# A third dA buffer, a different access pattern for two silu passes, and new due times in the scan stage of a four-layer image kernel

## The chip, the cores and the metric

The kernel runs as one program on one core of a Trainium2 chip. The metric is the device time of one execution in microseconds. Three runs of the kernel before took 7575.3, 7574.78 and 7561.64 us; the median is 7574.78 us.

The engines are named as in the profile: PE (TensorE, matrix products into PSUM), DVE (VectorE), ACT (ScalarE), POOL (GpSimd) and SP (SyncE, which here only issues DMAs). Each engine works through its own instructions in order.

## The reference

Four layers act on an image batch of 4 x 64 x 128 x 128 in float32. Layers 0 to 2 (a spectral gate with attention, a Fourier mixing block with experts, a Hartley convolution with blur) are not touched. Layer 2 ends with a mask that leaves 65 of the 128 columns nonzero. Layer 3 runs two selective scans over the result, one along the whole image ("spa", 65536 steps), one over the channels of each pixel ("spe", 8 steps for each of 65536 pixels), normalises each by groups, and adds them to the input:

```python
xi, z = split(x @ in_w.T)
xc = silu(conv(xi) + conv_b)
dt, B, C = split(xc @ xproj_w.T);  dt = softplus(dt @ dt_w.T + dt_b)
dA = exp(dt[..., None] * A);  dBx = dt[..., None] * B * xc[..., None]
h = dA_t * h + dBx_t          # scan over t, 16 states for each of 128 channels
y = sum_s(h * C_t) + xc * D
out = (y * silu(z)) @ out_w.T
...
spa = silu(group_norm(ys)) + x;  spe = x + silu(group_norm(ye))
return spa * w[0] + spe * w[1] + x
```

## The kernel before

Layer 3 is cut into chunks: 65 "spe" chunks of 512 tokens (64 pixels by 8 steps), one short chunk ("run") that follows the scan through 60 zero inputs, and 4 x 19 "spa" chunks of up to 483 tokens (7 image rows of 69 columns: 65 kept ones, and four in which the run of masked columns is held as constants). Every chunk has eight steps, one for each row group q, in the order `ORDER = (0, 2, 4, 6, 1, 3, 5, 7)`; the place of a group in it is called k below. A row group puts 16 channels x 8 states on the 128 partitions; the other 8 states lie behind them in the free dimension (`sg` 0 and 1).

One step is: two exponentials on ACT write dA (`do_exp`, L1490); the product of dt, x and B is written into the tile `hd` (`do_dB`, L1518), by DVE for k = 0, 2, 3, 5, 7 and by POOL for k = 1, 4, 6; DVE scans `hd` in place with dA (`do_scan`, L1525 for spe, L1529 and L1535 for spa); POOL multiplies the result with C (`do_hc`, L1564; in spe one instruction for two steps). PE sums the products over the states into the PSUM tile `ps_y` (`do_sums`), and once for each chunk DVE multiplies this with silu(z) (`do_y`, L1605).

dA has two buffers, both in PSUM and each of two banks; they alternate from step to step (`self.turn`). With two banks for the tile `m`, one for `y` and one for `dx`, PSUM is full.

Work of a chunk that comes ahead of its steps: `do_x` (L1415 to L1417) makes xc and zs by two silu passes, which need another table of ACT's functions than the exponentials, so a table load stands in front of them and another behind them. In spe chunks PE writes the result by steps, and the silu passes read PSUM in order and write SBUF with a step of 8 elements. `do_dt` computes softplus on ACT and PE, `do_bc` and `do_keep` make B and C, `do_put` and `do_copy` send dt and dt*x through DRAM to spread the rows over the partitions. The tiles xc and zs have three buffers each.

In spa chunks, the scan overwrites the columns of `hd` that stand for the masked run, and `keep_run` (L1680 to L1682, on ACT) writes them back from the saved tile `e_run`, in two pieces: k = 0 to 3 and k = 4 to 7.

From the second image on, eight spa chunks of each image also carry a part of the previous image's `combine`: DMAs in, two silu passes in place (part 1, L1819 and L1820), matmuls that add the three terms, copies out of PSUM and DMAs out; the last image's combine follows the scans. `affine` prepares its factors once for each image.

The order on PE, DVE, ACT and POOL is written out by hand: `scans` gives every piece of work a due time in steps (8 to a chunk, relative to the chunk's first step), sorts by it and emits in this order. A piece due at 2.3 stands on each engine behind all pieces due earlier. The DMA issues on SP are placed by the compiler's scheduler. Waits follow from the data: who reads a tile waits for its writer, and who writes a buffer waits for its last reader.

Of the kernel before, what the change touches and what calls it, by code (L numbers as in the profile page):

```python
# [9 lines left out]
F32 = mybir.dt.float32  # L10
# [27 lines left out]
ORDER = (0, 2, 4, 6, 1, 3, 5, 7)  # L38
BY_DVE = (0, 4, 6, 3, 7)


# [273 lines left out]
class Net:  # L315
# [944 lines left out]
    def layer3(self, x2s, x2k, y1, ye):  # L1260
        tc, nc = self.tc, self.nc
        self.x2s, self.x2k, self.y1, self.ye = x2s, x2k, y1, ye
        with ExitStack() as ctx:
# [7 lines left out]
            nc.vector.memset(self.eps, 1e-5)  # L1271
            self.dA = [self.psum.tile([128, 1024], F32, name=f"dA{i}") for i in range(2)]
            self.const, self.small = const, pool("st", 2)
            self.work = pool("w", 2)
# [128 lines left out]
    def do_x(self, u):  # L1403
        nc, c, n = self.nc, u["c"], u["n"]
        spa = u["spa"]

        v = lambda t: t if spa else t.rearrange("p (t x) -> p t x", t=8)
        w = lambda t: t if spa else t.rearrange("p (x t) -> p t x", t=8)
        a0, a2 = u["taps"]
        p, pz = self.ps("m")[:, u["lo"] : n], self.ps("m")[:, u["lo"] : n]  # L1410
        self.mm(v(p), c["w0"], a0, stop=False)
        self.mm(v(p), c["w1"], a2, start=False)
        self.mm(v(pz), c["z"][64:128], a2[64:128])
        u["xc"], u["zs"] = self.tile2("xc", u, 3), self.tile2("zs", u, 3)
        nc.scalar.activation(w(u["xc"]), v(p), AF.Silu, bias=c["cb"])  # L1415
        nc.scalar.activation(w(u["zs"]), v(pz), AF.Silu)
        nc.scalar.preload_act_table_set("natural_log_exp_and_others")  # L1417
# [62 lines left out]
    def do_exp(self, u, q, sg):  # L1480

        t = (lambda x: x) if u["spa"] else (lambda x: x.rearrange("p (x t) -> p x t", t=8)[:, :, 1:8])
        a = u["c"]["a"][:, 2 * q + sg : 2 * q + sg + 1]
        if sg == 0:
            self.turn = 1 - self.turn
            u["dA", q] = self.dA[self.turn]
        at = (TOK + 1) * sg + 1 if u["spa"] else 512 * sg
        if u["kind"] == "run" and sg == 0 and q in ORDER[:2]:
            self.nc.vector.memset(u["dA", q][:, TOK + 1 : TOK + 2], 0.0)
        self.nc.scalar.activation(t(u["dA", q][:, at + u["lo"] : at + u["n"]]), t(u["dt", q]), AF.Exp, scale=a)  # L1490
# [180 lines left out]

    def keep_run(self, u, part):

        at = slice(4 * part, 4 * part + 4)
        runs = lambda sg: self.all[:, at, (TOK + 1) * sg + TOK + CW :: CW][:, :, :CR]
        if u["kind"] == "run":
            for sg, to in ((0, self.e_run[:, at]), (1, runs(1))):
                of = (TOK + 1) * sg + RUN
                of = self.all[:, at, of : of + 1]
                self.nc.scalar.copy(to, of.to_broadcast([128, 4, CR]) if sg else of)  # L1680
        self.nc.scalar.copy(runs(0), self.e_run[:, at].to_broadcast([128, 4, CR]))  # L1681

    def scans(self, us):
# [7 lines left out]
        for ci, u in enumerate(us):  # L1691
            do = lambda when, f, *a: todo.append((8 * ci + when, len(todo), f, a))
            spa = u["spa"]
            if spa:
                do(-22.0, self.spa_load, u)
            else:
                for part, when in enumerate((-2.9, 4.7, 6.42)):
                    do(when, self.do_first, u, part)
                m, i = divmod(u["at"], 4)
                do(-13.0, self.spe_taps, u)  # L1700
                for g in range(8 if i == 0 else 0):

                    if m:
                        do(-48.0 + 3 * g if m > 1 else -48.0, self.spe_load, m, g)
                for g in range(8 if i == 3 or u["at"] == chunks - 1 else 0):
                    do(12.3 + 3 * g, self.spe_store, m, g)
            do(-12.9, self.do_x, u)
            for part, when in enumerate((-11.65, -11.25, -10.65, -10.05, -9.8, -9.55, -9.3, -9.0, -8.05)):
# [6 lines left out]
            for i, when in enumerate((4.7, 4.74, 5.9, 9.42, 9.74) if u["kind"] != "run" else ()):  # L1715
                do(when, self.do_sums, u, i)
            for part in range(2 if spa else 0):
                do(4.1 * part + 4.6, self.keep_run, u, part)
            if u["kind"] != "run":
                do(10.76, self.do_y, u)  # L1720
                do(12.2, self.spa_out if spa else self.spe_out, u)
                do(13.64, self.do_stats, u)
        mine = [j for j in range(len(steps)) if not by_pool(j)]
        for j, (u, q) in enumerate(steps):
            do = lambda when, f, *a: todo.append((j + when, len(todo), f, a))
            do(-6.0, self.do_copy, u, q, "dt")
            do(-1.3, self.do_exp, u, q, 0)
            do(-1.0, self.do_exp, u, q, 1)
            if by_pool(j):
                do(-6.5, self.do_copy, u, q, "dx")  # L1730
                do(-4.22, self.do_dB, u, q, nc.gpsimd)
            else:
                do(-1.61, self.do_dB, u, q, nc.vector)
            do(0.3, self.do_scan, u, q)
            if u["kind"] != "run":
                do(0.77, self.do_hc, u, q)
# [4 lines left out]
        for ci, u in enumerate(us):  # L1741
            if u["kind"] == "spa" and u["at"][1] == SPC - 1:
# [3 lines left out]
                for i in range(8):  # L1746

                    for part, when in enumerate((4.0, 10.37, 16.3, 16.75, 16.8, 17.51)):
                        do(when + 8 * (i + 1), self.combine, b, i, part)
# [118 lines left out]
```

## Time and profile before

| what | value |
|---|---|
| median of three runs | 7574.78 us |
| the profiled execution's own time | 7564.79 us |
| its span, first to last instruction | 7562.9 us |
| busy share of the span: PE, DVE, ACT, POOL | 88%, 71%, 64%, 47% |
| granted TensorE clock, mean | 0.94 |
| first and last `do_y` (L1605) | 3640.58 and 7499.20 us |
| mean distance of two `do_y`, spe chunks | 27.33 us |
| the same, full spa chunks without combine | 26.37 us |
| the same, spa chunks with combine | 29.56 us |

The scan stage takes the second half of the span. `do_y` occurs once in each chunk, so the distance of two of its starts is the time of one chunk; the means are over 61 spe chunks (3640.58 to 5307.50 us), 36 spa chunks without and 24 with combine. The page's busy shares are averages over the whole span, most of POOL's work lies in this stage. Start-to-start distances are used for the cost of one instruction where they stand back to back, since neighbouring instructions overlap by a few hundredths of a microsecond.

### The profile page before, as it was taken

What the parts mean: (1) busy time and instruction counts of PE and PEld (TensorE: products, weight loads), DVE (VectorE), ACT (ScalarE), POOL (GpSimd) and SP (SyncE); (2) the same over time, 40 slices, a digit from 0 to 9 for tenths busy, and PEclk for the clock granted to TensorE, in tenths of its full rate; (3) what the DMA queues carried; (4) which work ended last, traced back from release to release, by engine and by line L of the source; (5) the groups of instructions that cost most, each with busy time, mean ns of one, the idle gap of its engine ahead of it and who ended that gap; (6) DMA issues with size and microseconds to landing.
All of it is one profiled execution on the core that took longest, in us unless ns stands there. A gap on an engine that the chain in (4) does not pass through costs nothing.

```text
span 7562.9 us, 105294 instructions
## 1 busy us (share of the span) xinstructions
PE 6622.1 (88%) x39058; PEld 2887.9 (38%) x39058; DVE 5344.1 (71%) x6633; ACT 4813.2 (64%) x7926; POOL 3524.4 (47%) x1648
## 2 busy tenths in 40 slices
PE   7998999989998999989888888888888788788786
PEld 6334553446334643446222222222222232232233
DVE  2665646563665556553898998889888888888886
ACT  2565536553655446443777777777777777787885
POOL 1000000000000000000899999999899789788795
PEclk9998999998998999988999999999999999999998
DMA  3000010001000200013455555554444454554554
GB/s 87 1 1 1 28 46 1 1 28 45 1 1 1 63 10 1 1 61 125 134 137 140 138 139 139 140 139 137 132 136 136 135 158 131 144 160 124 149 154 115
DMA packets 364098, 646.93 MB, mean 86 GB/s; under 512 B 46784, under 2 KB 219584, under 8 KB 362048
## 3 DMA queue, kind: packets, MB, share of 16 engines
q1 hardware_dynamic: 357680, 609.91, 29.1%
q10 hardware_dynamic: 5904, 30.28, 1.2%
q8 instruction: 308, 5.05, 0.3%
q14 instruction: 206, 1.69, 0.1%
HBM read 517.80 MB, written 122.22 MB: 85 GB/s over the span
## 4 chain that ended last, share of the span: by engine, by line
PE 56%; DVE 19%; ACT 11%; issue 7%; POOL 4%; DMA 3%; SPq 0%; DVEq 0%; POOLq 0%; ACTq 0%
PE ps_sp L333 13%; PE ps_m L333 12%; PE ps_s L333 7%; PE ps_o L333 6%; PE ps_dx L333 6%; DVE hd L1518 5%; DVE hd L1525 5%; PE ps_pt L333 4%; PE ps_y L333 4%; ACT dA L1490 3%; DVE hd L1529 3%; POOL hc L1564 2%; DMA big<-in_sr 2%; DVE big L1061 2%; ACT L1417 1%
## 5 line engine op out<-in xcount | busy, mean ns | idle before, releaser
L1564 POOL TENSOR_TENSOR hc<-hd,C 128x910 f32<-128x910 f32 (+3 forms) x868 | 2316.0, 2677 | 362.3 <-DVE hd L1529 147.5
L1529 DVE TENSOR_TENSOR_SCAN hd<-dA,hd 128x968 f32<-128x968 f32 (+1 forms) x576 | 1226.3, 2131 | 188.7 <-ACT dA L1490 185.9
L755 DVE TENSOR_REDUCE nmz<-ps_sp 128x1 f32<-128x320 f32 x2048 | 896.0, 485 | 621.6 <-PE ps_sp L333 612.4
L333 PE MATMUL ps_dx<-dtx,c_sel 128*128 128x483 f32 (+3 forms) x1420 | 796.1, 644 | 589.9 <-DVE hd L1518 589.5
L771 ACT ACTIVATE big<-ps_sp 128x512 f32<-128x512 f32 (+1 forms) x1536 | 830.6, 592 | 719.6 <-PE ps_sp L333 718.3
L1525 DVE TENSOR_TENSOR_SCAN hd<-dA,hd 128x1024 f32<-128x1024 f32 x520 | 1185.2, 2283 | 109.7 <-ACT dA L1490 100.5
L930 POOL TENSOR_TENSOR aw<-pack_a 128x128 f32<-128x128 f32 x8 | 3.5, 454 | 2192.4 <-PE ps_m L333 2192.4
L1518 POOL TENSOR_TENSOR hd<-s_dx,B 128x1024 f32<-128x1024 f32 (+5 forms) x450 | 956.4, 2126 | 95.1 <-ACT hd L1681 78.5
L333 PE MATMUL ps_sp<-uT,kT 32*128 32x512 f32 x3072 | 923.9, 648 | 1.4 <-ACT big L771 0.8
L1518 DVE TENSOR_TENSOR hd<-ps_dx,B 128x1024 f32<-128x1024 f32 (+5 forms) x750 | 810.9, 1081 | 33.2 <-PE ps_dx L333 31.7
L333 PE MATMUL ps_sp<-kT,qT 32*128 32x320 f32 x4096 | 817.4, 499 | 3.9 <-ACT qT L736 3.3
L1490 ACT ACTIVATE dA<-s_dt,c_spa_a 128x483 f32<-128x483 f32 (+3 forms) x1232 | 788.9, 645 | 44.9 <-DVE hd L1529 30.6
L1490 ACT ACTIVATE dA<-s_dt,c_spe_a 128x448 f32<-128x448 f32 x1040 | 652.0, 637 | 63.3 <-DVE hd L1525 51.5
L333 PEld LDWEIGHTS ps_dx<-dtx,c_sel 128*128 128x128 f32 x1420 | 230.8, 195 | 1079.5 <-DVE hd L1518 586.6
L333 PE MATMUL ps_y<-hc,c_sum 128*32 128x455 f32 (+3 forms) x4512 | 548.6, 556 | 3.2 <-POOL hc L1564 3.2
L333 PEld LDWEIGHTS ps_sp<-uT,kT 32*128 32x128 f32 x3072 | 278.8, 185 | 438.0 <-issue 242.7
L333 PE MATMUL ps_o<-big,va 128*32 128x512 f32 (+1 forms) x3072 | 414.3, 611 | 0.0
L333 PE MATMUL ps_s<-pack_a,big 128*64 128x128 f32 (+4 forms) x2832 | 371.6, 307 | 43.7 <-DMA big<-in_x 20.2
L333 PEld LDWEIGHTS ps_sp<-kT,qT 32*128 32x128 f32 x4096 | 358.2, 190 | 57.2 <-issue 36.6
L333 PEld LDWEIGHTS ps_s<-pack_a,big 128*128 128x128 f32 (+2 forms) x2832 | 330.0, 180 | 65.6 <-issue 26.2
L333 PE MATMUL ps_m<-xc,c_spa_bc 128*128 128x483 f32 (+3 forms) x616 | 313.1, 631 | 0.0
L1461 ACT COPY C<-ps_m 128x483 f32<-128x483 f32 (+4 forms) x284 | 159.5, 562 | 211.7 <-PE ps_m L333 210.9
(405 smaller groups left out, 10180.6 us busy)
## 6 DMA issues: line engine op xcount, KB each, us to landing
s_dt<-ddt SPq DMA_DIRECT2D x520, 256.0 KB
s_dt<-ddt SPq DMA_DIRECT2D x544, 241.5 KB
s_dx<-ddx SPq DMA_DIRECT2D x195, 256.0 KB
s_dx<-ddx SPq DMA_DIRECT2D x204, 241.5 KB
ddt<-dt SPq DMA_DIRECT2D x65, 256.0 KB
ddx<-dtx SPq DMA_DIRECT2D x65, 256.0 KB
A<-x2s SPq DMA_DIRECT2D x136, 121.2 KB
ddt<-dt SPq DMA_DIRECT2D x68, 241.5 KB
```

What stands on the lines that cost most here:

```text
L333: self.nc.tensor.matmul(out, lhsT, rhs, start=start, stop=stop)
L755: nc.vector.tensor_reduce(self.nmz[n % 2][:, j, at : at + 1], p[:, :KEYS], AX.X, ALU.max, negate=True)
L771: nc.scalar.activation(slot(m, 2 * wu + q)[rows], p[rows], AF.Exp)
L930: nc.gpsimd.tensor_tensor(aw[i], k(f"aw{i + 1}"), k("sg"), ALU.mult)
L1061: nc.vector.scalar_tensor_tensor(acc(i), y, gate[:, p : p + 1], acc(i), ALU.mult, ALU.add)
L1417: nc.scalar.preload_act_table_set("natural_log_exp_and_others")
L1461: self.nc.scalar.copy(u["BC"][k // 2][:, k % 2, u["lo"] : u["n"]], u["bc", k])
L1490: self.nc.scalar.activation(t(u["dA", q][:, at + u["lo"] : at + u["n"]]), t(u["dt", q]), AF.Exp, scale=a)
L1518: eng.tensor_tensor(v(dB[:, :, x:y]), v(d), v(u["BC"][0][:, :, x:y]), ALU.mult)
L1525: scan(hd[:, :1024], dA, hd[:, :1024], 0.0, ALU.mult, ALU.add)
L1529: scan(hd[:, :m], dA[:, :m], hd[:, TOK : TOK + m], 0.0, ALU.mult, ALU.add)
L1564: mul = lambda to, a, b: self.nc.gpsimd.tensor_tensor(to, a, b, ALU.mult)
```

## The change

A third dA buffer, in SBUF, is used at k = 4 (q = 1) alone; the other seven steps alternate between the two PSUM buffers, and the exponentials of k = 4 are emitted 0.95 steps earlier. In spe chunks the two silu passes write SBUF in order and read PSUM with a step of 64 elements. `do_x` is due 0.8 steps earlier, directly behind part 1 of `combine`, which is moved by 0.08 steps. `keep_run` has three pieces (k = 0-1, 2-4, 5-7) due at 2.6, 6.0 and 9.0 instead of two due at 4.6 and 8.7. `do_y` is due 0.57 steps later, the output matmul and copy 0.35 steps later, the output's DMAs of spe 0.35 later.

```diff
+AHEAD = 4
+KEEP = ((0, 2, 2.6), (2, 5, 6.0), (5, 8, 9.0))
...
             self.dA = [self.psum.tile([128, 1024], F32, name=f"dA{i}") for i in range(2)]
+            self.dA.append(const.tile([128, 1024], F32, name="dA2"))
...
-        w = lambda t: t if spa else t.rearrange("p (x t) -> p t x", t=8)
+        w = lambda t: t if spa else t.rearrange("p (t x) -> p x t", t=8)
+        o = lambda t: t if spa else t.rearrange("p (x t) -> p x t", t=8)
...
-        nc.scalar.activation(w(u["xc"]), v(p), AF.Silu, bias=c["cb"])
-        nc.scalar.activation(w(u["zs"]), v(pz), AF.Silu)
+        nc.scalar.activation(o(u["xc"]), w(p), AF.Silu, bias=c["cb"])
+        nc.scalar.activation(o(u["zs"]), w(pz), AF.Silu)
...
         if sg == 0:
-            self.turn = 1 - self.turn
-            u["dA", q] = self.dA[self.turn]
+            k = ORDER.index(q)
+            self.turn = self.turn if k == AHEAD else 1 - self.turn
+            u["dA", q] = self.dA[2 if k == AHEAD else self.turn]
...
-    def keep_run(self, u, part):
+    def keep_run(self, u, k0, k1):
...
-                do(-13.0, self.spe_taps, u)
+                do(-13.8, self.spe_taps, u)
...
-                    do(12.3 + 3 * g, self.spe_store, m, g)
-            do(-12.9, self.do_x, u)
+                    do(12.65 + 3 * g, self.spe_store, m, g)
+            do(-13.7, self.do_x, u)
...
-            for part in range(2 if spa else 0):
-                do(4.1 * part + 4.6, self.keep_run, u, part)
+            for k0, k1, when in KEEP if spa else ():
+                do(when, self.keep_run, u, k0, k1)
             if u["kind"] != "run":
-                do(10.76, self.do_y, u)
-                do(12.2, self.spa_out if spa else self.spe_out, u)
+                do(11.33, self.do_y, u)
+                do(12.55, self.spa_out if spa else self.spe_out, u)
...
-            do(-1.3, self.do_exp, u, q, 0)
-            do(-1.0, self.do_exp, u, q, 1)
+            early = 0.95 if j % 8 == AHEAD else 0.0
+            do(-1.3 - early, self.do_exp, u, q, 0)
+            do(-1.0 - early, self.do_exp, u, q, 1)
...
-                    for part, when in enumerate((4.0, 10.37, 16.3, 16.75, 16.8, 17.51)):
+                    for part, when in enumerate((4.0, 10.29, 16.3, 16.75, 16.8, 17.51)):
```

## The prediction

> **What bounds the kernel now.** I read the page's busy shares by slices first, since the change touches the scan stage alone, then busy times by window, then the chain of waits inside the stage, then single chunks on the timeline.
>
> ```profile
> DVE  2665646563665556553898998889888888888886
> ACT  2565536553655446443777777777777777787885
> POOL 1000000000000000000899999999899789788795
> ```
>
> From slice 20 on, DVE and POOL are both eight to nine tenths busy, ACT seven. The windows give busy microseconds (and instructions) of PE, PEld, DVE, ACT and POOL in 200 us of spe, of spa with combine and of plain spa:
>
> ```profile
> 3900.00:4100.00 200.00, 170.03 (x632) 57.28 (x632) 181.76 (x120) 153.20 (x235) 182.30 (x66) 0.97 0.52 141
> ...
> 6500.00:6700.00 200.00, 172.99 (x623) 65.90 (x625) 162.78 (x127) 168.17 (x264) 167.67 (x82) 0.94 0.62 170
> 6700.00:6900.00 200.00, 169.22 (x594) 56.99 (x590) 176.99 (x116) 157.31 (x269) 185.85 (x91) 0.96 0.50 141
> ```
>
> No engine is full: POOL and DVE lack a tenth each, in combine chunks a sixth. The waits of the stage say what for (total us, times, longest):
>
> ```profile
> DVE hd L1529 <- ACT dA L1490: 185.9, 200, 2.9
> DVE yz L1605 <- PE ps_y L333: 181.5, 139, 3.5
> ...
> POOL hc L1564 <- DVE hd L1529: 147.5, 162, 11.5
> ACT hd L1681 <- POOL hd L1518: 112.3, 65, 2.9
> POOL hc L1564 <- DVE hd L1525: 95.7, 54, 3.3
> DVE hd L1525 <- ACT dA L1490: 95.0, 133, 2.3
> ...
> POOL hd L1518 <- ACT hd L1681: 78.5, 60, 2.7
> ```
>
> So DVE waits for exponentials and for the y sums, and POOL waits for DVE and for keep_run. On the DVE timeline two such places of one spe chunk:
>
> ```profile
> 4412.54 2.29 DVE L1525 TENSOR_TENSOR_SCAN hd<-dA,hd 128x1024 f32<-128x1024 f32 x1 [0.83 <-ACT dA L1490]
> ...
> 4433.84 0.69 DVE L1605 TENSOR_TENSOR yz<-ps_y,zs 128x512 f32<-128x512 f32 x1 [2.00 <-PE ps_y L333]
> ```
>
> The first is the scan of k = 5, behind the silu passes and their two table loads on ACT. In a combine chunk there are four loads:
>
> ```profile
> 6599.91 1.28 ACT L1819 ACT_TABLE_LOAD   x1
> ...
> 6602.78 1.28 ACT L1490 ACT_TABLE_LOAD   x1
> 6604.07 1.37 ACT L1490 ACTIVATE dA<-s_dt,c_spa_a 128x483 f32<-128x483 f32 x2
> 6605.46 1.28 ACT L1415 ACT_TABLE_LOAD   x1
> ```
>
> **The change part by part.**
>
> *Silu passes in spe.* 1.198 and 1.138 us today. What costs is the write with a step: copies of 128x512 that scatter single words into SBUF took 1.05 us (L341, b = 1), plain ones 0.585. Reads of PSUM with a step are free in the nearest rows: 0.577 us for 512 at a step of 8 (L1647), 0.372 us for 256 at a step of 128 (L341), as much as 256 in order (L1208, 0.372). So I take 0.68 (L1428, same size, pointer bias) and 0.59; were the step of 64 not free, 1.2 each. ACT gains 1.07 us in each of 65 chunks.
>
> *Silu passes together.* Part 1 of combine at 2.29 and do_x at 2.3 have no exponential between them, so two of four loads go: 2 x 1.283 = 2.57 us in 24 chunks. Combine chunks take 29.56 us against 26.37, and DVE waits 2.88 us there for dA behind these loads (6610.59). I count the loads in full: 26.99 us. Hidden, they would be worth 0; with the exponentials' delay, the whole difference of 3.19.
>
> *keep_run in three.* One more ACT copy of 0.24 us in 76 chunks, beside an ACT with a fifth idle. POOL's dB of k = 1 no longer waits for the first piece, now two steps earlier, and the last piece no longer covers k = 4, whose dB POOL writes just before. Both waits above (78.5 and 112.3 us) should go; the first piece now stands before the exponentials of k = 5 and waits for POOL's hc of k = 1, due 0.83 steps ahead of it; the old first piece stood as far behind hc of k = 3, so I count nothing. If POOL lags by more, ACT and scan 5 wait with it.
>
> *dA at k = 4 in SBUF, and early.* The exponentials of k = 3 and 4 now precede the silu block, so DVE has two scans in hand while ACT is in it, and k = 5 to 6 find their PSUM buffer free one scan earlier. An exponential into SBUF costs the same (L1431, 512 elements, 0.625 us). The 0.83 and the like should go. But this scan has both inputs in SBUF, which no other large DVE instruction of the stage has. The trace shows what this does beside POOL in two tiny ones of affine:
>
> ```profile
> 6460.55 2.18 DVE L364 TENSOR_TENSOR gn_dv<-mv,gn_mean 128x1 f32<-128x1 f32 x1
> 6462.76 1.12 DVE L366 SCALAR_TENSOR_TENSOR gn_q<-gn_dv,mv 128x1 f32<-128x1 f32 x1
> ...
> 6460.51 2.20 POOL L1518 TENSOR_TENSOR hd<-s_dx,B 128x952 f32<-128x952 f32 x1
> 6462.67 1.20 POOL L1450 TENSOR_TENSOR dtx<-dt,xc 128x483 f32<-128x483 f32 x1
> ```
>
> One column takes 0.16 and 0.22 us elsewhere; here each ends when POOL's instruction ends. So scan 4 will wait for the instruction that POOL has under way: between 0 and 4.04 us in spe (hc), 2.17 in spa. Whether POOL then waits for the scan is not seen (POOL's dtx kept its 1.20): 0 at the one end, a whole scan (2.20 us start to start in spe, 2.08 in spa) at the other. I take the whole scan, since what is seen of the other side is a full block. The Trainium skill (SBUF — State Buffer, Who interferes with whom) says that a DVE instruction with two SBUF inputs and a GpSimd instruction that reads SBUF exclude each other, the second to come blocked until the first is through; the DVE half agrees with the 2.18 us, the POOL half no row here shows. By it the sum is the forecast below, and with the row's half alone nearer the first rival.
>
> *do_x earlier, do_y later.* The y sums have 0.57 steps more, and yz comes behind scan 3: the waits of 0.43 and 2.00 us should go. But the new zs takes the third-last chunk's buffer, whose reader is that very yz: zs, due at 2.3, waits for yz, due at 3.33, that is for scan 3. Behind zs on ACT: a load, exponentials 5, softplus; DVE's scan 5 waits for those. From the end of scan 3: yz 0.61, zs 0.59, load 1.28, exponentials 1.31, in all 3.8 us; DVE meanwhile has yz 0.61, dB 1.11 and scan 4 2.20, in all 3.9. So nothing, while yz is on time and scan 4 covers it; where yz is late, all of it counts. On PE do_x's six matmuls pass no other work and wdt passes ow (1.1 us each); SP's row and store DMAs follow their producers, at half of the DMA time; do nothing.
>
> *The sum*, by POOL, which becomes the bound. Spe: 4 hc x 4.04 + 3 dB x 2.32 + dtx 1.24 + bb 0.61 = 24.97, with the blocked scan 27.17, against 27.33: -0.16 x 65 = -10. DVE needs 8 x 2.20 + 5 x 1.11 + 1.2 (yz, y0, stats) = 24.3, with 0.5 for ps_dx 24.8, so it can give scan 4 up to 2.4 us of waiting. Plain spa: 8 x 2.10 + 3 x 2.17 + 1.17 = 24.48, with the scan 26.56, against 26.37: +0.19 x 36 = +7. Combine: -2.57 x 24 = -62. POOL will not be without gaps: the tightest chunks now (25.13 us, plain spa) hold 0.65 us; I take half, 0.33 x 101 chunks = +33. Together -32 us. The profiled execution took 7564.8 us, 10 below the median of the runs: 7533 us, 0.55% below that median.
>
> **The rivals.**
>
> *POOL isn't held by the scan* (and DVE's wait falls in slack). Then POOL needs 24.97 and 24.48, plus the 0.65: spe 25.6, -1.71 x 65 = -111; plain 25.13, -1.24 x 36 = -45; combine 26.1 with its copies of 0.96 on DVE, -3.46 x 24 = -83. Sum -239: 7326 us. For it: no POOL instruction in the trace is lengthened. Against: DVE's is, to the very end.
>
> *DVE's wait at scan 4 makes DVE the bound*, the one that ends slower. If scan 4 meets the start of an hc in spe each time, it waits 4.04: 24.8 + 4.04 = 28.84, +1.51 x 65 = +98; spa as in the sum, (0.19 + 0.33) x 36 = +19, combine -62. Sum +55: 7620 us. It decides from a mean wait of 2.5 us on, where 24.8 passes 27.33. For it: hc of k = 3 becomes ready just when scan 3 ends, 1.7 us ahead of scan 4. Against: a late DVE meets a POOL that is further on.
>
> *The wait of zs for yz takes the place of the old ones.* If yz stays 2.0 us late in every other spe chunk, ACT is held by as much and scan 5 with it: +66 on the forecast, 7599 us. Against: yz comes 2.2 us later and the sums are done by then.
>
> *The silu passes gain nothing* by the new order: 1.07 us more of ACT in 65 chunks, within its idle time; no time of its own.
>
> **How the numbers follow.** About 0.2% (15 us) is what a measurement can tell here. Forecast 0.44 (its own range 7495 to 7560), POOL not held 0.20, DVE bound 0.22, zs 0.14. Faster: 0.20 and nearly nine tenths of 0.44, 0.59; within 0.2%: what is left of it and the low edge of zs, 0.09; slower 0.32. The range goes from near the first rival to past the second: 7340 to 7630.
>
> **What would show it.** Scans at L1530 with dA2 of 3 to 6 us, ending with a POOL instruction, and POOL gaps of 2 us beside them; xc and zs at 0.68 and 0.59 us; no load between combine's silu and xc; 26.6 to 27.5 us from one yz to the next. Wrong: scans of dA2 at 2.28 us beside a busy POOL, spe chunks over 28 us, or zs waiting for yz longer than before with scan 5 late behind it.

## The result and the profile after

The changed kernel takes 7619.66 us (median of 8 runs, 7595.25 to 7634.48) against 7573.7 us for the kernel before on the same chip (8 runs). The ratio is 1.006, 95% interval 1.0044 to 1.0075: slower by 0.6%, where 0.55% faster was forecast. The profiled execution took 7634.48 us, 69.7 us more than the profiled one of before. The medians differ by 46 us: the profiled execution of before lies 9 us below its median and that of the changed kernel 15 us above, so about a third of the 69.7 us is spread between executions.

The mean distances of two `do_y` say where. Spe chunks went from 27.33 to 28.68 us, plain spa chunks from 26.38 to 27.27, combine chunks from 29.56 to 27.49. Times 65, 36 and 24 chunks that is +88, +32 and -50, together +70 us, about the difference of the two profiled executions (the chunks at the ends of the stretches, which these means leave out, change it by a few us).

The page's busy shares by slices, changed kernel:

```profile
DVE  3665546564666356544999999999888899889896
ACT  2565446553665355434676776666777787777774
POOL 1000000000000000001999999999889899898895
```

DVE is busier than before in the spe half of the stage (slices 20 to 27), though the instructions are the same; POOL stands at nine tenths there before and after. The windows (busy us and instructions of PE, PEld, DVE, ACT and POOL, then clock and DMA) for spe, spa with combine and plain spa:

```profile
3900.00:4100.00 200.00, 168.77 (x627) 56.09 (x625) 184.74 (x118) 144.70 (x230) 194.44 (x66) 0.98 0.51 138
6500.00:6700.00 200.00, 164.18 (x603) 63.20 (x604) 169.08 (x164) 151.42 (x267) 166.94 (x93) 0.91 0.54 149
6700.00:6900.00 200.00, 171.38 (x609) 62.15 (x611) 179.62 (x122) 153.49 (x267) 183.31 (x89) 0.95 0.56 158
```

In spe POOL is busy for 194 of 200 us, with as many instructions as before (66) in 182 us. They became longer; the granted clock did not fall (0.97 before, 0.98 now). The groups of the large DVE and POOL instructions of the spe chunks (3640 to 5300 us; count, busy us, mean ns, idle time before them), before:

```profile
L1525 DVE TENSOR_TENSOR_SCAN hd<-dA,hd 128x1024 f32<-128x1024 f32 x488 | 1112.6, 2283 | 100.0 <-ACT dA L1490 91.0 <-POOL hd L1518 7.5
...
L1564 POOL TENSOR_TENSOR hc<-hd,C 128x1792 f32<-128x1792 f32 x244 | 998.1, 4091 | 137.8 <-DVE hd L1525 91.5 <-PE ps_dx L333 37.1 <-PE ps_m L333 3.4
L1518 POOL TENSOR_TENSOR hd<-s_dx,B 128x1024 f32<-128x1024 f32 x182 | 431.6, 2371 | 0.0
```

and after:

```profile
L1530 DVE TENSOR_TENSOR_SCAN hd<-dA,hd 128x1024 f32<-128x1024 f32 x464 | 1172.0, 2540 | 122.5 <-ACT dA L1495 122.4
...
L1569 POOL TENSOR_TENSOR hc<-hd,C 128x1792 f32<-128x1792 f32 x232 | 1013.1, 4373 | 108.3 <-DVE hd L1530 85.7 <-PE ps_m L335 22.5
L1523 POOL TENSOR_TENSOR hd<-s_dx,B 128x1024 f32<-128x1024 f32 x174 | 448.5, 2578 | 0.0
```

Only one scan in eight, that of k = 4 (scan 4 below), has both inputs in SBUF, and no other scan of a spe chunk is longer than 2.3 us, so DVE waits for POOL inside it by 8 x (2540 - 2283) ns = 2.06 us a chunk on average. POOL's instructions gain 4 x 282 + 3 x 207 ns = 1.75 us a chunk. The waits of the stage (us in total, times, longest):

```profile
ACT dt L1448 <- PE ps_m L335: 425.0, 135, 5.4
DVE hd L1534 <- ACT dA L1495: 187.3, 129, 4.1
DVE hd L1530 <- ACT dA L1495: 131.5, 115, 3.7
...
ACT xc L1419 <- PE ps_m L335: 115.1, 109, 2.6
...
ACT hd L1686 <- POOL hc L1569: 10.4, 8, 3.2
...
DVE yz L1610 <- PE ps_y L335: 5.1, 3, 2.4
ACT zs L1420 <- DVE yz L1610: 4.5, 7, 0.8
```

Those of `yz` (181.5 us before) and of keep_run (112.3 and 78.5) are gone, as intended. DVE's waits for exponentials are not (95.0 in spe before, 131.5 now), and ACT's wait for PE at the copy of dt out of PSUM has doubled:

```profile
ACT dt L1444 <- PE ps_m L333: 219.7, 135, 4.6
```

### The profile page after: what moved, and what is told of

Its sections match the earlier page's. It is cut to its first block, busy times and chain, and to the rows that moved or that the text cites. A ratio compares the mean times of both kernels' runs of the same rounds, so it can differ in the third digit from the quotient of the medians.

```text
span 7632.7 us, 104968 instructions
## 1 busy us (share of the span) xinstructions
PE 6634.6 (87%) x39058; PEld 2903.7 (38%) x39058; DVE 5552.4 (73%) x6635; ACT 4680.6 (61%) x7957; POOL 3675.5 (48%) x1648
## 4 chain that ended last, share of the span: by engine, by line
PE 58%; DVE 15%; issue 10%; ACT 9%; POOL 5%; DMA 2%; SPq 0%; POOLq 0%; DVEq 0%; ACTq 0%
PE ps_m L335 14%; PE ps_sp L335 13%; PE ps_s L335 7%; PE ps_o L335 6%; PE ps_dx L335 5%; DVE hd L1523 5%; PE ps_pt L335 4%; PE ps_y L335 4%; POOL hc L1569 4%; DVE hd L1534 3%; ACT dA L1495 3%; DVE big L1063 1%; DVE hd L1530 1%; ACT L1421 1%; PE ps_m L786 1%
## 5 line engine op out<-in xcount | busy, mean ns | idle before, releaser
L1569 POOL TENSOR_TENSOR hc<-hd,C 128x910 f32<-128x910 f32 (+3 forms) x868 | 2424.7, 2806 | 362.1 <-DVE hd L1534 124.8
L1534 DVE TENSOR_TENSOR_SCAN hd<-dA,hd 128x968 f32<-128x968 f32 (+1 forms) x576 | 1316.0, 2301 | 187.8 <-ACT dA L1495 187.3
L1530 DVE TENSOR_TENSOR_SCAN hd<-dA,hd 128x1024 f32<-128x1024 f32 x520 | 1311.8, 2537 | 138.0 <-ACT dA L1495 137.9
L1523 POOL TENSOR_TENSOR hd<-s_dx,B 128x1024 f32<-128x1024 f32 (+5 forms) x450 | 998.8, 2220 | 17.5 <-DMA s_dx<-ddx 6.3
L335 PE MATMUL ps_y<-hc,c_sum 128*32 128x455 f32 (+3 forms) x4512 | 626.8, 586 | 16.0 <-POOL hc L1569 15.9
L1448 ACT COPY dt<-ps_m 128x512 f32<-128x512 f32 (+3 forms) x142 | 80.0, 563 | 441.8 <-PE ps_m L335 441.5
## 6 DMA issues: line engine op xcount, KB each, us to landing
s_dt<-ddt SPq DMA_DIRECT2D x520, 256.0 KB
s_dx<-ddx SPq DMA_DIRECT2D x195, 256.0 KB
ddt<-dt SPq DMA_DIRECT2D x65, 256.0 KB
ddx<-dtx SPq DMA_DIRECT2D x65, 256.0 KB
```

Of the source, the lines that this page charges most:

```text
L335: self.nc.tensor.matmul(out, lhsT, rhs, start=start, stop=stop)
L1448: nc.scalar.copy(u["dt"], u["v"])
L1523: eng.tensor_tensor(v(dB[:, :, x:y]), v(d), v(u["BC"][0][:, :, x:y]), ALU.mult)
L1530: scan(hd[:, :1024], dA, hd[:, :1024], 0.0, ALU.mult, ALU.add)
L1534: scan(hd[:, :m], dA[:, :m], hd[:, TOK : TOK + m], 0.0, ALU.mult, ALU.add)
L1569: mul = lambda to, a, b: self.nc.gpsimd.tensor_tensor(to, a, b, ALU.mult)
```

## The experiments

Four theories are named in the expectations. L: the scan with both inputs in SBUF and POOL's instructions keep each other off. Z: zs waits for `yz`, the last reader of its buffer. M: do_x stands too early, so that ACT reaches the silu passes before PE has made their input. N: joining the silu passes is itself the loss. The edits of the change were taken apart; each row is one run, the last three columns the mean us from one `do_y` to the next. These columns come from the profiled execution, which can lie some tens of us from the median (35 us above it in e17, 30 in e4, 21 in e16), so small differences between rows of them say little.

| run | median us | ratio to before, 95% | spe | combine | plain spa |
|---|---|---|---|---|---|
| kernel before | 7573 | | 27.33 | 29.56 | 26.38 |
| changed kernel | 7619.66 | 1.0044 to 1.0075 | 28.68 | 27.49 | 27.27 |
| e1 changed, no third buffer | 7945.97 | 1.0471 to 1.0502 | 30.03 | 30.91 | 30.67 |
| e2 third buffer alone | 7725.32 | 1.0185 to 1.0219 | 30.03 | 27.22 | 27.10 |
| e3 silu pattern alone | 7572.31 | 0.9987 to 1.0006 | 27.32 | 29.89 | 26.29 |
| e4 due times alone | 7887.03 | 1.0387 to 1.0443 | 29.68 | 30.93 | 30.65 |
| e8 silu passes joined alone | 7511.44 | 0.9902 to 0.9931 | 27.29 | 27.20 | 26.29 |
| e9 e8, silu pattern, keep_run | 7509.88 | 0.9897 to 0.9927 | 27.32 | 27.27 | 26.35 |
| e10 SBUF operand at k = 4 | 7781.88 | 1.0260 to 1.0292 | 30.14 | 29.84 | 26.84 |
| e11 SBUF operand at k = 7 | 7683.38 | 1.0126 to 1.0160 | 27.42 | 30.68 | 27.87 |
| e12 do_y late alone | 7585.64 | 1.0007 to 1.0025 | 27.86 | 29.64 | 26.31 |
| e13 do_x early alone | 7803.44 | 1.0290 to 1.0321 | 29.78 | 29.79 | 27.79 |
| e14 changed, no third buffer, exponentials early | 7710.07 | 1.0166 to 1.0200 | 29.09 | 27.73 | 28.09 |
| e15 changed, do_x late | 7615.58 | 1.0035 to 1.0068 | 28.35 | 27.30 | 27.21 |
| e16 changed, dt copy late | 7528.39 | 0.9922 to 0.9962 | 27.76 | 27.49 | 26.64 |
| e17 third buffer and do_y late | 7599.01 | 1.0020 to 1.0049 | 28.77 | 27.09 | 27.34 |
| e18 e15 and e16 together | 7532.51 | 0.9936 to 0.9966 | 27.51 | 27.38 | 26.69 |
| e19 e9 and dt copy late | 7487.49 | 0.9878 to 0.9911 | 27.25 | 27.32 | 25.98 |

### Taking the change apart: e1 to e4

**e1**: the changed kernel without the third buffer and without the early exponentials.

```diff
-            self.dA.append(const.tile([128, 1024], F32, name="dA2"))
...
-            self.turn = self.turn if k == AHEAD else 1 - self.turn
-            u["dA", q] = self.dA[2 if k == AHEAD else self.turn]
+            self.turn = 1 - self.turn
+            u["dA", q] = self.dA[self.turn]
...
-            early = 0.95 if j % 8 == AHEAD else 0.0
+            early = 0.0
```

> The changed kernel with the third dA buffer undone: two PSUM buffers alternate over all eight steps and the exponentials of k = 4 stand where they stood; the silu access patterns, all due times and the three keep pieces stay. Theory L (the scan with both inputs in SBUF and POOL shut each other out): the changed kernel's trace has k = 4 scans of up to 9.6 us and POOL instructions lengthened by 2.0 us; without them spe falls to about 26.4 us a chunk, plain spa to 25.9, combine stays near 27: 7574 - 60 - 17 - 62 = 7435 us (7400 to 7500), and no scan is longer than 2.4 us. Rival Z (zs waits for yz, which now stands behind scan 3): the slow spe chunks stay, 7580 to 7620 us.

It lost far more than the changed kernel, +373 us, where L had forecast a gain. Three ACT lines of one of its spe chunks (start, us, instruction, idle time before it):

```profile
4306.29 1.28 ACT L1418 ACT_TABLE_LOAD   x1
4310.01 0.69 ACT L1418 ACTIVATE xc<-ps_m,c_spe_cb 128x512 f32<-128x512 f32 x1 [2.43 <-PE ps_m L335]
...
4312.97 2.54 ACT L1493 ACTIVATE dA<-s_dt,c_spe_a 128x448 f32<-128x448 f32 x4
```

ACT has loaded the silu table and then stands for 2.43 us, because PE makes do_x's input last; the exponentials of k = 4 and 5 are queued behind. `xc` waits 249.0 us in this kernel, `zs` 2.8 us for `yz`. This is theory M, formed here.

**e2**: the kernel before with the third buffer and the early exponentials only.

```diff
+            self.dA.append(const.tile([128, 1024], F32, name="dA2"))
...
+            self.turn = self.turn if k == AHEAD else 1 - self.turn
+            u["dA", q] = self.dA[2 if k == AHEAD else self.turn]
...
+            early = 0.95 if j % 8 == AHEAD else 0.0
```

> The kernel before with the third dA buffer in SBUF at k = 4 and its early exponentials, and nothing else. Theory L: the whole price and little of the gain, POOL's floor 27.2 us in spe and 26.6 in spa with DVE's waits on top: 28.5 to 29 us a spe chunk, 7640 to 7720 us. Rival Z: this part is a gain (DVE waits for dA, 95 and 186 us in all, shrink), 7450 to 7560 us.

Slower by 2%: +2.70 us a spe chunk, +0.72 in plain spa, but -2.34 in combine chunks. That last figure was not foreseen, and the trace says where it comes from. ACT in a combine chunk of this kernel:

```profile
6716.47 1.28 ACT L1823 ACT_TABLE_LOAD   x1
...
6718.52 0.81 ACT L1824 ACTIVATE xht<-xht,t,s 128x520 f32<-128x520 f32 x1
6719.35 0.66 ACT L1417 ACTIVATE xc<-ps_m,c_spa_cb 128x483 f32<-128x483 f32 x1
...
6720.94 1.28 ACT L1419 ACT_TABLE_LOAD   x1
```

Two loads, not four: the only exponentials that stood between combine's part 1 (due at 2.37) and do_x (3.1) were those of k = 4 (2.7 and 3.0), and 0.95 steps earlier they stand ahead of both. So the early exponentials join the passes by themselves; at the line of the exponentials the stage has 3 loads here and 27 in the kernel before.

**e3**: the silu access pattern only (the hunk of `do_x` in the diff).

> The kernel before with the silu passes of spe reading PSUM in steps and writing SBUF in order, and nothing else. Both theories: xc 0.68 and zs 0.59 us, 1.07 us of ACT in each of 65 chunks, ahead of the exponentials that the k = 5 scan waits for (0.83 us there): -0.4 to -0.8 us a chunk, 7520 to 7550 us; spa unchanged.

No difference, where both theories had 7520 to 7550 us. The passes did become shorter, xc from a mean of 1198 to 687 ns, zs from 1138 to 598:

```profile
L1416 ACT ACTIVATE xc<-ps_m,c_spe_cb 128x512 f32<-128x512 f32 x61 | 41.9, 687 | 50.3 <-PE ps_m L333 50.1
```

**e4**: the due times of do_x, do_y, outputs, stores, taps and combine only (the hunk of `scans` without keep_run and the exponentials).

> The kernel before with the due times alone: do_x at -13.7 beside combine's silu passes at 10.29, do_y at 11.33, the output at 12.55, the stores at 12.65. Theory L: combine chunks lose two table loads, 29.6 to 27.0 us, -62 us, and yz no longer waits for the y sums in spe (1.1 us a chunk, some of it kept): 7470 to 7530 us. Rival Z: zs behind yz holds ACT and the k = 5 scan, spe chunks over 28 us, which eats the 62 us and more: 7580 to 7640 us.

+314 us, outside both forecasts, so the due times are the larger part of what the third buffer and the early exponentials cover in the changed kernel; `xc` waits 233.5 us for PE here. The granted clock of PE is lower in e1 and e4 (means 0.908 and 0.916, against 0.940 before), and whether that is a cause or a consequence of a part of their loss is not shown; e13 below has the early do_x, and a loss, at 0.940.

### The join and keep_run: e8 and e9

**e8** joins the silu passes the other way, by moving combine's part 1 behind the old do_x.

```diff
-                    for part, when in enumerate((4.0, 10.37, 16.3, 16.75, 16.8, 17.51)):
+                    for part, when in enumerate((4.0, 11.09, 16.3, 16.75, 16.8, 17.51)):
```

> The kernel before with one number changed: part 1 of combine is due at 11.09 instead of 10.37, directly ahead of do_x, which stays at -12.9 behind the exponentials of k = 4. Theory M (the due times cost because do_x at 2.3 brings ACT to the silu passes before PE has their input, with the exponentials of k = 4 queued behind them): the silu passes share their table loads without that, 2.57 us in 24 combine chunks: 29.6 to 27.0 us, 7500 to 7525 us in all, plain and spe chunks unchanged. Rival N (joining the silu passes is itself the loss, 4 us of ACT in one piece): combine chunks stay at 29 us or above, 7570 or more.

7572.0 to 7511.4 us: one number gives -61 us, and combine chunks -2.36 us each. N falls, and the chunk gains nearly the price of two loads (2.57 us).

**e9** adds the silu pattern and the three pieces of keep_run to e8.

> The kernel before with combine's silu passes at 11.09, the silu access patterns of spe and keep_run in three pieces; no third buffer, do_x and do_y where they were. Theory M: the join's gain, plus what keep_run's waits (78 us of POOL, 112 us of ACT) hid in spa chunks, some 0.3 to 0.6 us in each of 60: 7465 to 7510 us. Rival N: no better than the kernel before.

-1.6 us against e8, which is nothing. The waits between keep_run and POOL's dB are gone here too, but ACT now waits 83.7 us in the stage for POOL's hc at keep_run (3.3 us in the kernel before), the risk that the prediction had named. The change without the third buffer, the early exponentials and the moved do_x and do_y, joined from the other side, is 0.9% faster than before.

### The SBUF operand by itself: e10 and e11

**e10** puts dA of k = 4 into SBUF and changes nothing in the order; k = 4 merely doesn't use its PSUM buffer. **e11** does the same at k = 7.

```diff
+            self.dA.append(const.tile([128, 1024], F32, name="dA2"))
...
-            u["dA", q] = self.dA[self.turn]
+            u["dA", q] = self.dA[2 if ORDER.index(q) == AHEAD else self.turn]
```

> The kernel before with dA of k = 4 in an SBUF buffer of its own and every instruction where it was: the PSUM buffers alternate as before and the exponentials are not early, so only the operand's place changes. Theory L (DVE's scan with both inputs in SBUF and POOL shut each other out): POOL loses 2.0 to 2.3 us a chunk, DVE waits up to 4 us and more at this scan; spe 27.3 to 29 or 30 us, plain spa 26.4 to 27, 7650 to 7750 us. Rival (the loss of the third buffer alone is one of order, not of the port): 7550 to 7590 us, scans of k = 4 at 2.28 us.

> The same as the run with k = 4 in place, but for k = 7, the scan for which POOL sits idle in spe (1.1 to 2.9 us before the hc of k = 6 and 7 in the trace of before). Theory L: POOL has little to lose there and DVE little to wait for, so less than half of the loss of k = 4 in spe (28 us or less a chunk); in spa, where POOL's hc of k = 6 runs beside the scan of k = 7, about as at k = 4. In all 7590 to 7660 us. Rival (the SBUF operand costs the same wherever it stands): as at k = 4.

e10: +210 us, nearly all in spe (+2.81 us a chunk). The groups in spe show both halves of the lock, DVE 2640 ns (2283) and POOL's dB 2931 (2371):

```profile
L1527 DVE TENSOR_TENSOR_SCAN hd<-dA,hd 128x1024 f32<-128x1024 f32 x442 | 1162.3, 2640 | 119.9 <-ACT dA L1492 116.8 <-POOL hc L1566 3.1
...
L1520 POOL TENSOR_TENSOR hd<-s_dx,B 128x1024 f32<-128x1024 f32 x166 | 486.6, 2931 | 0.0
```

e11: in spe +0.1 us. Scan 7 waits 8 x (2385 - 2283) ns = 0.82 us a chunk (mean of the scans 2385 ns), and no POOL instruction is longer (2372 ns):

```profile
L1520 POOL TENSOR_TENSOR hd<-s_dx,B 128x1024 f32<-128x1024 f32 x182 | 431.7, 2372 | 0.0
```

In spa the same edit costs 1.1 us (combine) and 1.5 us (plain), where e10 costs 0.3 and 0.5; L had put them about equal there, and 7683 us is above its range. L holds, and its price depends on where the scan stands, from 0.1 to 2.8 us a chunk.

### The due times one by one: e12 to e15

**e12**: do_y, outputs and stores later, nothing else. **e13**: do_x, taps and combine's part 1 earlier, nothing else.

```diff
...
-                do(10.76, self.do_y, u)
-                do(12.2, self.spa_out if spa else self.spe_out, u)
+                do(11.33, self.do_y, u)
+                do(12.55, self.spa_out if spa else self.spe_out, u)
```

> The kernel before with one part of the due times alone: do_y 0.57 steps later, the output matmul, copy and spe stores 0.35 later; do_x stays where it was. Theory M (all of the +313 us of the due times comes from do_x standing ahead of PE's input for it): no loss here, spe chunks 27.0 to 27.5 us, 7540 to 7580 us. Theory Z (zs is due at 3.1 and its buffer's last reader yz now at 3.33, so ACT waits for DVE): a loss, spe 27.8 us or more, 7600 us or more, with ACT zs waiting for DVE yz in the chain of waits.

```diff
...
-            do(-12.9, self.do_x, u)
+            do(-13.7, self.do_x, u)
...
```

> The kernel before with the other part of the due times alone: do_x and its taps 0.8 steps earlier, combine's part 1 0.08 earlier; do_y stays. Theory M: most of the +313 us, 7800 to 7900 us, spe 29 to 29.7 us, plain spa 30 us or more, and ACT's xc waits for PE's ps_m by 1 to 2.5 us a chunk. Theory Z (do_x alone is harmless, since yz still precedes zs): 7500 to 7580 us.

e13 falls where M put it in all, +231 us, and `xc` waits 256.0 us in the stage; plain spa chunks, at 27.79 us, are below M's 30. e12 is neither: +13 us, spe +0.53, DVE's waits for `yz` gone and its waits for exponentials up from 91.0 to 193.4 us in spe, with no `zs` waiting for `yz`.

**e14**: e1 with the early exponentials left in, so that they go into the PSUM buffer that scan 2 reads.

```diff
...
-            self.turn = self.turn if k == AHEAD else 1 - self.turn
-            u["dA", q] = self.dA[2 if k == AHEAD else self.turn]
+            self.turn = 1 - self.turn
+            u["dA", q] = self.dA[self.turn]
...
```

> The changed kernel without the third buffer, with the exponentials of k = 4 still 0.95 steps early; they go into the PSUM buffer whose reader is the scan of k = 2. It keeps the order of ACT and takes away the SBUF operand alone. If the loss of the changed kernel is the scan with both inputs in SBUF (L): DVE's scan 4 falls to 2.2 us and POOL's instructions beside it to 4.1, spe 27.2 to 27.6 us, and the time to 7500 to 7550 us, 70 to 120 below the changed kernel. If it is the early do_x (M): the early exponentials cover it as the third buffer did, and what is left of the loss, xc waiting for ps_m, stays: 7580 to 7640 us. If two buffers are not enough (exponentials of k = 4 then wait for scan 2, and the silu block behind them): 7700 us or more.

7710 us, in the range named for two buffers being too few and far from L's 7500 to 7550. But ACT's exponentials wait only 13 us in the stage for scans to free their buffer. What is long is ACT's wait for `yz`; here, and only here, Z is seen (elsewhere it is 6.4 us at most):

```profile
ACT zs L1419 <- DVE yz L1608: 231.5, 133, 3.2
```

So this run took the SBUF operand away and brought another wait in; it decides nothing on L.

**e15**: the changed kernel with do_x and taps at their old due times, and the passes still joined.

```diff
...
-            do(-13.7, self.do_x, u)
+            do(-12.9, self.do_x, u)
...
-                    for part, when in enumerate((4.0, 10.29, 16.3, 16.75, 16.8, 17.51)):
+                    for part, when in enumerate((4.0, 11.09, 16.3, 16.75, 16.8, 17.51)):
```

> The changed kernel with do_x and its taps back at their old due times and combine's part 1 0.8 steps later than in the changed kernel, so that the silu passes stay joined. M with the third buffer in place: xc's wait for ps_m (115 us of the stage) goes, 7540 to 7590 us. If the third buffer already hides that wait (L alone is left): 7600 to 7640 us, spe 28.4 to 28.9. If the early do_x is what brings scan 4 to a better place beside POOL than in the third buffer alone (spe 30.0 there): 7660 to 7740 us, spe 29.5 to 30.

-4 us, within the spread of the runs. So in the changed kernel the early do_x costs nothing, M is not its loss, and L is what is left. The wait of `xc` did not go with the move (105.3 us in the stage against 115.1); e2, with do_x at its old place, has 123.6, so beside the SBUF scan PE is late for do_x wherever do_x stands. But e15 and e2 both hold the SBUF scan, and are 28.35 and 30.03 us a spe chunk. Setting DVE's time apart explains the order (spe, us a chunk; the wait inside scan 4, in e11 inside scan 7, is 8 x (mean of the scans - 2283 ns), idle is all idle time before DVE's instructions):

| run | chunk | wait in scan 4 | idle before instructions | rest |
|---|---|---|---|---|
| before | 27.33 | 0 | 2.71 | 24.6 |
| changed | 28.68 | 2.06 | 2.16 | 24.5 |
| e2 | 30.03 | 2.79 | 2.86 | 24.4 |
| e10 | 30.14 | 2.86 | 2.82 | 24.5 |
| e11 (scan 7) | 27.42 | 0.82 | 2.07 | 24.5 |
| e15 | 28.35 | 1.54 | 2.30 | 24.5 |
| e16 | 27.76 | 1.32 | 1.81 | 24.6 |
| e17 | 28.77 | 2.02 | 2.18 | 24.6 |

The rest is DVE's own work. If idle time could absorb the wait inside scan 4, the idle column would fall by as much; in the changed kernel it fell by 0.55 of 2.06 us, in e2 and e10 not at all. At k = 7 it did: 0.64 of 0.82 us, so the edit is nearly free there. (The next two expectations give the waits in scan 4 as 2.5 us for the changed kernel and 3.4 for e2; by the means of the scans they are 2.06 and 2.79.)

### Where the wait comes from and where it goes: e17 and e16

**e17**: e2 with do_y, outputs and stores late, as in e12.

> The kernel before with the third buffer, the early exponentials of k = 4 and the later do_y, outputs and stores; do_x, combine, silu and keep_run as before. It differs in do_y's place alone from the run with the third buffer alone, where scan 4 waits 3.4 us a chunk for POOL in spe and a chunk takes 30.0 us. If the loss follows the place where scan 4 meets POOL (yz then stands between scan 3 and scan 4 and puts scan 4 off): its mean wait falls to 1.7 to 2.5 us, spe 28.3 to 28.8 us, 7600 to 7650 us. If the loss with the third buffer alone comes of something else that do_x, silu or keep_run mended: spe stays at 29.7 or more, 7700 us or more.

7725 to 7599 us, the wait in scan 4 from 2.79 to 2.02 us. So the same move of do_y that alone cost 13 us is worth 126 us beside the SBUF scan. `yz` (0.6 us) then stands between scan 3 and scan 4 and puts scan 4 at another point of POOL's order. Counted over the 61 chunks, the shorter wait in scan 4 is half of the 1.26 us that a spe chunk gains (0.63 us); DVE's idle time fell by as much (0.60), about what `yz` had waited for the sums in e2 (0.68).

**e16** asks what the wait does afterwards. A stretch of one timeline of the changed kernel, all engines:

```profile
4245.92 8.25 DVE L1530 TENSOR_TENSOR_SCAN hd<-dA,hd 128x1024 f32<-128x1024 f32 x2
...
4249.79 4.37 POOL L1523 TENSOR_TENSOR hd<-s_dx,B 128x1024 f32<-128x1024 f32 x1
...
4254.09 1.19 DVE L1523 TENSOR_TENSOR hd<-ps_dx,B 128x1024 f32<-128x1024 f32 x1
...
4255.34 1.12 PE L335 MATMUL ps_dx<-dtx,c_sel 128*128 128x512 f32 x2 [1.88 <-DVE hd L1523]
...
4257.28 1.12 PE L335 MATMUL ps_m<-sp_c,xht 128*128 128x512 f32 x2
...
4261.02 0.59 ACT L1448 COPY dt<-ps_m 128x512 f32<-128x512 f32 x1 [2.87 <-PE ps_m L335]
...
4261.50 0.64 ACT L1495 ACTIVATE dA<-s_dt,c_spe_a 128x448 f32<-128x448 f32 x1
...
4262.18 2.29 DVE L1530 TENSOR_TENSOR_SCAN hd<-dA,hd 128x1024 f32<-128x1024 f32 x1 [1.21 <-ACT dA L1495]
```

Read downwards: scans 4 and 5 take 8.25 us instead of 4.46, since scan 4 waits for POOL; POOL's dB is held for 2.0 us. DVE's next dB is late, and it is what frees the one bank of `ps_dx`. PE waits 1.88 us for it, with do_dt's matmuls in its queue behind. ACT waits 2.87 us for these at the copy of dt, with the second exponential of k = 0 behind the copy. DVE waits 1.21 us for that exponential. The wait has gone round four engines and come back to DVE. Over 61 spe chunks of each run (us a chunk) the end of this path appears with the SBUF scan at k = 4, and not with that at k = 7:

| run | DVE idle before scan 0 | before scan 1 | before scans 5 and 6 | ACT idle before the dt copy |
|---|---|---|---|---|
| before | 0.25 | 0 | 1.40 | 1.85 |
| e11 (k = 7) | 0.01 | 0 | 1.38 | 1.87 |
| e10 (k = 4) | 2.11 | 0 | 0.09 | 3.77 |
| e2 | 2.04 | 0 | 0.12 | 3.68 |
| changed | 1.65 | 0 | 0.34 | 3.36 |
| e16 | 0 | 1.47 | 0.12 | 3.19 |

The wait in scan 4 does use up the idle time before scans 5 and 6, and brings as much or more of it back before scan 0. The experiment moves the copy behind that exponential; PE's and DVE's orders stay as they are:

```diff
...
-            for part, when in enumerate((-11.65, -11.25, -10.65, -10.05, -9.8, -9.55, -9.3, -9.0, -8.05)):
+            for part, when in enumerate((-11.65, -11.25, -10.65, -10.05, -9.8, -9.55, -9.3, -8.95, -8.05)):
...
```

> The changed kernel with one number altered: ACT's copy of dt out of PSUM is due 0.05 steps later, so that it stands behind the second exponential of k = 0 instead of ahead of it. That copy waits 195 us for PE in the spe chunks (113 us before), and scan 0 behind it then waits for dA. If the waits of DVE for exponentials behind this copy are what is left of the loss (DVE's 2.1 us a chunk of waiting for dA on top of 2.5 us of waiting for POOL): scan 0 no longer waits, spe 27.6 to 28.1 us, 7560 to 7590 us. If POOL, held by the scan, is the bound (27.1 us of work a chunk) or the same wait only goes over to the next scan: 7605 to 7640 us, spe 28.4 to 28.9.

7528.39 us, 91 us below the changed kernel and below both forecasts, with a spe chunk of 27.76. The scans in spe:

```profile
L1530 DVE TENSOR_TENSOR_SCAN hd<-dA,hd 128x1024 f32<-128x1024 f32 x481 | 1163.0, 2448 | 94.7 <-ACT dA L1495 92.5
```

Scan 0 no longer waits, but the wait is not gone. It stands one scan on, at k = 1, whose exponentials are now the first behind the copy:

```profile
4240.01 0.64 ACT L1495 ACTIVATE dA<-s_dt,c_spe_a 128x448 f32<-128x448 f32 x1
...
4244.98 0.58 ACT L1448 COPY dt<-ps_m 128x512 f32<-128x512 f32 x1 [4.33 <-PE ps_m L335]
...
4249.03 2.29 DVE L1530 TENSOR_TENSOR_SCAN hd<-dA,hd 128x1024 f32<-128x1024 f32 x1 [1.90 <-ACT dA L1495]
```

So one number did not break the loop. All idle time of DVE fell from 2.16 to 1.81 us a chunk, and the wait inside scan 4 from 2.06 to 1.32: the larger part of the 0.92 us is that scan 4 waits less (counted over the 61 chunks, 0.66 us, and 0.30 of idle time). POOL's hc and dB are as much longer as in the changed kernel (1.89 us a chunk against 1.75), and POOL's gaps shrink from 1.87 to 0.79 us. So the hold of POOL is not what bounded the changed kernel, which left POOL those 1.87 us. That the loop through DVE, PE and ACT is what keeps DVE's idle time from absorbing the wait is read from the stretch and the table; no run removes it with the SBUF scan in place.

### Does it add, and is it a remedy: e18 and e19

**e18** is e15 with the dt copy late, **e19** is e9 with the dt copy late (the same one number in both).

> The changed kernel with do_x late again (as in the run of that name) and the dt copy 0.05 steps later (as in the run of that name). If the two gains add: spe 27.3 to 27.5 us, 7500 to 7525 us, with DVE's wait at scan 4 below 1.5 us a chunk. If the dt copy's place was the whole of it: 7520 to 7550 us, spe 27.6 to 27.9.

> The kernel without the third buffer, with combine's part 1 late, the silu access pattern and keep_run in three pieces, and the dt copy 0.05 steps later. Its DVE waits 72 us in spe for exponentials, but in the stretch read (4240 to 4270 us) behind softplus at k = 6, not behind the dt copy: 7495 to 7515 us, spe 27.1 to 27.4. If the dt copy's place is worth something without the SBUF scan too: 7440 to 7480 us, spe 26.3 to 26.9. This run is also the candidate for a version below both kernels.

e18: 7532.5 us. A late do_x adds nothing in time, as it added nothing in e15. e19: 7487.5 us, the fastest kernel of the study, 1.1% below before (ratio 0.9894) and 132 us below the changed kernel. Against e9 the dt copy gives 22 us there (the two intervals to before overlap), in plain spa (26.35 to 25.98) and hardly in spe (27.32 to 27.25), as DVE's waits for exponentials in spe arise elsewhere. With the SBUF scan it gives 91 (e16) and 83 us (e18 against e15). Most of its gain comes with the SBUF scan, and the kernel is still faster without that scan: the third buffer costs, and nothing that it brings is missed once the passes are joined by e8's number.

## Why the prediction was wrong

*Silu passes in spe*: right. 0.69 and 0.60 us against 0.68 and 0.59, hidden on ACT, worth nothing (e3).

*Silu passes together*: right in size, -2.57 forecast, -2.36 alone (e8), -2.07 in the changed kernel, and no load is left between the passes. ACT in a combine chunk of the changed kernel:

```profile
6601.40 1.28 ACT L1825 ACT_TABLE_LOAD   x1
...
6603.45 0.81 ACT L1826 ACTIVATE A<-A,t,s 128x520 f32<-128x520 f32 x1
6604.28 0.66 ACT L1419 ACTIVATE xc<-ps_m,c_spa_cb 128x483 f32<-128x483 f32 x1
...
6605.87 1.28 ACT L1421 ACT_TABLE_LOAD   x1
```

What the step missed is that the early exponentials alone take the same two loads away (e2).

*keep_run in three*: right. Its two waits went (in e9 another came, ACT's for hc), and no time came of it (e9).

*dA at k = 4 in SBUF*: the mechanism was right on both sides: scan 4 waits for POOL, and POOL is held by it. The hold is 1.75 us a chunk in spe where a whole scan, 2.20, was taken; start to start POOL's work is 28.68 - 1.87 (its gaps) = 26.8 us a chunk, against 27.17 forecast.

*do_x earlier, do_y later*: "the waits of 0.43 and 2.00 us should go" holds (`yz` waits 5.1 us in all). "do nothing", said of do_x's place on PE, is wrong by itself, +231 us in e13, since no one asked when PE would get to do_x's matmuls. In the changed kernel it holds (e15), where the exponentials of k = 3 and 4 are made ahead of do_x; that this is the reason is argued, since e14, which has them early too, is slow by another wait.

*The sum* failed here, in two sentences that are one mistake. "It can give scan 4 up to 2.4 us of waiting" took all idle time of DVE as free to absorb a wait. "I take half, 0.33" took POOL's gaps from the tightest chunks. Measured, POOL's gaps in spe are 108.3 / 58 = 1.87 us a chunk, mostly waiting for DVE's scans; DVE waits 2.06 us in scan 4 and still 2.16 elsewhere. The missing question was the one that the prediction asked of ACT but not of PE: who waits for the work behind scan 4? That is scan 5, dB of k = 7, then PE's `ps_dx`, do_dt's matmuls, the dt copy, the exponentials of k = 0. In numbers, a spe chunk was to become -0.16 + 0.33 = 0.17 us longer and became 1.35 us longer: 65 x 1.18 = 77 us. Plain spa was to be 0.52 longer and is 0.89: 13 us. Combine chunks are shorter by 2.07 instead of 2.57: 12 us. Together 102 us, the distance from 7533 to the profiled 7634.5.

In spa the working failed as well: it had POOL held for a whole scan (2.08 us). In the full spa chunks, plain and combine together, POOL's hc became longer by 64 ns each (2140 to 2204), 0.5 us a chunk, and dB not at all (2219 and 2221 ns). It is DVE that waits, 8 x (2345 - 2167) ns = 1.4 us in scan 4.

*The rivals.* "POOL isn't held by the scan" fell with e10's 2931 ns. "zs waits for yz" fell with 4.5 us of such waits. "DVE's wait at scan 4 makes DVE the bound" gave 7620 us, and 7619.66 came. That agreement is luck: the sum was for the profiled execution, which took 7634.5, and its price for a spe chunk was near by two errors that cancel: it took 4.04 us of waiting and 0.5 us of other idle time, and the runs show 2.06 and 2.16. Its point of decision, 2.5 us, was too high: at 2.06 the kernel is slower. By an estimate from the table above, with DVE idle for 2.2 us elsewhere, a chunk passes 27.33 at about 27.33 - 24.5 - 2.2 = 0.6 us.

With one copy on ACT a place later (e16), the same kernel runs at 7528 us. That does not make the forecast right: scan 4 still waits 1.32 us a chunk there and DVE is idle for 1.81 elsewhere, terms that the sum left out. Why scan 4 meets POOL so that it waits 2.06 us in one order and 1.32 in the other stays open.

## What to carry to other kernels

Idle time of an engine is not by itself a reserve that a new wait can use up: at k = 7 it took in 0.64 of 0.82 us, at k = 4 in place nothing of 2.86. Follow the instruction behind the delayed one to who reads its result or gets its buffer, through that engine's queue, until the chain ends in slack or comes back; here, as far as the stretch and the waits show, it came back in four steps. When an operand moves to a memory that two engines contend for, price it by the place where it meets the other engine: the same edit cost 0.1 us a spe chunk at k = 7 and 2.8 at k = 4. And try each due time alone: one number (e8) gained 61 us where the whole change lost 46, and another (e16) turned the sign of the change.

## What the runs showed of the hardware that was not expected

DVE is not always served when POOL's instruction ends. In six of 58 spe chunks of the changed kernel it was passed over by two or three POOL instructions that stood back to back. DVE and POOL in one of them:

```profile
3755.40 11.75 DVE L1530 TENSOR_TENSOR_SCAN hd<-dA,hd 128x1024 f32<-128x1024 f32 x2
...
3755.81 4.08 POOL L1569 TENSOR_TENSOR hc<-hd,C 128x1792 f32<-128x1792 f32 x1
3759.84 2.38 POOL L1523 TENSOR_TENSOR hd<-s_dx,B 128x1024 f32<-128x1024 f32 x1
3762.17 0.65 POOL L1554 TENSOR_TENSOR bb<-B,C 128x128 f32<-128x128 f32 x1
...
3767.22 4.07 POOL L1569 TENSOR_TENSOR hc<-hd,C 128x1792 f32<-128x1792 f32 x1 [4.41 <-DVE hd L1530]
```

The pair of scans takes 11.75 us instead of 4.46, and runs only when POOL has nothing left; POOL then stands for 4.41 us, waiting for these scans. Where POOL loses, it is held for nearly the whole scan of 2.28 us (the dB at 4249.79 above: 4.37 us instead of 2.37). The Trainium skill (SBUF — State Buffer, Who interferes with whom) says that the two exclude each other and that the one that comes second is blocked until the first is through. The 4.37 us agree; the 11.75 us do not, since there the one that waited was blocked by instructions that came after it. What decides which of the two gets in between two instructions of POOL was not found.
